# Working out the next group's mean and deviation inside the last stage of the group before it

## The chip, the cores and the metric

The kernel runs on one core of one Trainium2 chip. The metric is the device time of one launch in microseconds (us), as a median of several runs.

## The reference

Four layers follow one another on a tensor of 16 images, 32 channels, 128 x 128, in single precision. Each adds to its input the result of one operation on the group-normalised input (16 groups of two channels per image):

```python
x = x + row_lstm(_gn(x), W2, b2, W1, b1)      # layer 0: 128 steps, one per diagonal
x = x + adder_conv(_gn(x), weight)            # layer 1: -sum |patch - w| over 32 channels x 9 taps, quantised
x = x + hartley(_gn(x), weights1)             # layer 2: 2-D Hartley transform, 32 x 32 modes mixed, and back
x = x + unet(_gn(x), conv1_w, ...)            # layer 3: 5 edge operators, 7 convolutions, 3 poolings, 3 deconvolutions

def _gn(v, G=16, eps=1e-5):                   # mean and variance over 2 channels x 128 x 128
    m = jnp.mean(g, axis=(2, 3, 4)); s = jnp.var(g, axis=(2, 3, 4))
    return (g - m) / jnp.sqrt(s + eps)
```

The change concerns the mean and the deviation that layer 2 uses, that is, `m` and `1/sqrt(s + eps)` of the output of layer 1.

## The kernel before, in words

`stage0` (L103) is layer 0. It ends about 650 us into the profiled execution. `rest` (L493) then runs three things in one stream of instructions.

The first is the adder convolution, `Differences.run` (L682). It goes over 16 images and two halves of each; a half takes 72 tiles of 128 x 8192 differences. A tile is made either on VectorE (DVE, `d_dve`, L760) or on ScalarE (ACT, `d_act`, L757), whichever would be free earlier by the planned durations `DVE_US` and `ACT_US` (L487), and TensorE (PE) sums it (L647). At the end of a half, `finish` (L624) adds the residual and writes the partial statistics `stat` (L630) that layer 2 needs; when both halves of an image `b` are stored, `weave.finished = b` (L636).

The second is the background: layers 2 and 3 for groups of four images, in `After.work` (L975). Group `g` may start when `weave.finished` has reached `4 * g + 3`. Its steps are `forward` (L1031: statistics, Hartley transform forward, mixing of the modes), `encoder` (L1511: `back`, which is the transform back; `statistics` of the edge operators; the folded table `wf` of the first convolution, L1545 to L1557; `conv1`, L1683; then small layers), and `last` (L1794: the last composed deconvolution, the multiplication by the residual, and the store of the output in 16 transfers per unit of rows, L1847).

These are Python generators, and the order of the instructions on every engine is fixed while the program is written. `Weave` (L351) holds a planned clock. A positive number yielded is planned TensorE time; a negative one is a wait of so many planned us before the generator goes on; `SUMMED` is a wait until the products before it are done. While such a wait runs, only adder tiles are put into the queues. `later` puts a step off by some planned us, `done` runs it at once. The queues themselves are in order: an instruction that has to wait for data holds up everything behind it on its engine, and the queue of SyncE (SP), which issues most transfers, runs as far ahead as its own waits let it.

The third is the end. After the last adder tile, `drain` (L455) interleaves what is left of group 2 (the first `Weave`, groups 0 to 2) with all of group 3 (a second `Weave` with its own memory and PSUM banks). Waits are stretched by 1.5 in it, until one of the two streams is through; the other is then `alone`.

At the boundary between two groups the planned waits are these. `last` ends with `yield -16.0` (L1879) and then stores whatever is not stored yet (L1880). `work` waits 8 more (L981). `forward` then zeroes `xs` on ACT (L1044), issues four loads of `xh` (L1053, 1 MB each), aggregates the statistics (L1059), and calls `normalised` (L780), which sends two tiny products through TensorE (L786, L795) and takes an inverse square root in 19 small VectorE instructions (L802 to L814). A third product (L1069) spreads the result over all partitions, two VectorE instructions (L1071, L1074) leave it in `mr`, and after `yield -4.0` (L1111) the first product of the transform (L1119) reads `xh`. `mr` is used by `scaled` (L1079, L1082).

Of the kernel before, what the change touches and what calls it, by code (L numbers as in the profile page):

```python
# [7 lines left out]
F32 = mybir.dt.float32  # L8
# [3 lines left out]
ALU = mybir.AluOpType  # L12
# [3 lines left out]
B, C, H, W = 16, 32, 128, 128  # L16
# [334 lines left out]
class Weave:  # L351
# [10 lines left out]
    def __init__(self, work):  # L362
        self.work, self.pending = work, None
        self.pe = self.dve = self.act = self.now = self.base = 0.0
        self.until = self.ready = 0.0
        self.draining = self.alone = False
        self.stretch = 1.0
        self.finished, self.count, self.put_off, self.for_act, self.ends = -1, 0, [], [], {}
# [121 lines left out]
SUMMED = ("summed",)  # L490
# [289 lines left out]
def normalised(nc, pool, ps, weave, mv, n, avg, eps, out):  # L780

    mean = pool.tile([128, n], F32, name="ns_mean")
    nc.vector.tensor_copy(mean, mv[:, :, 0])
    yield -2.0
    p = ps.tile([128, 512], F32, name="acc")
    nc.tensor.matmul(p[:, :n], avg, mean, start=True, stop=True)  # L786
    yield SUMMED
    nc.vector.tensor_copy(out[:, 0], p[:, :n])
    v = pool.tile([128, n], F32, name="ns_v")
    nc.vector.tensor_sub(v, mean, out[:, 0])  # L790
    nc.vector.tensor_mul(v, v, v)
    nc.vector.tensor_add(v, v, mv[:, :, 1])
    yield -2.0
    p = ps.tile([128, 512], F32, name="acc")
    nc.tensor.matmul(p[:, :n], avg, v, start=True, stop=True)  # L795
    yield SUMMED
    nc.vector.tensor_copy(v, p[:, :n])
    inv_sqrt_into(nc, pool, weave, out[:, 1], v, n, eps)
    yield -2.0


def inv_sqrt_into(nc, pool, weave, out, v, n, eps):  # L802

    a = pool.tile([128, n], F32, name="is_a")
    nc.vector.tensor_scalar(a, v, eps, None, ALU.add)
    i = pool.tile([128, n], I32, name="is_i")
    nc.vector.tensor_scalar(i, a.bitcast(I32), 1, None, ALU.arith_shift_right)
    nc.vector.tensor_scalar(i, i, -1.0, 1597463007.0, ALU.mult, ALU.add)
    y, t = i.bitcast(F32), pool.tile([128, n], F32, name="is_t")
    for k in range(4):  # L810
        nc.vector.tensor_mul(t, y, y)
        nc.vector.tensor_mul(t, t, a)
        nc.vector.tensor_scalar(t, t, -0.5, 1.5, ALU.mult, ALU.add)
        nc.vector.tensor_mul(out if k == 3 else y, y, t)  # L814
    weave.dve += 2.0
# [143 lines left out]
class After:  # L959


    def __init__(self, nc, tc, side, sm, ps, cst, bias, a, d, stat, out):
        self.nc, self.tc, self.side, self.ps, self.cst, self.bias = nc, tc, side, ps, cst, bias
        self.a, self.d, self.stat, self.out = a, d, stat, out
        self.spare, self.banks = None, 0
        self.buffers = {"t_x": 4, "xm": 3, "xw": 2, "t_w": 3, "t_r": 4, "frames": 2, "gm": 3, "e_v": 3, "l_x": 2}
        store = [d["up"][i] for i in range(3)]
        self.up5 = Composed(nc, sm, a, "deconv1", "conv5", bias[:, 7:8], bias[:, 4:5], store[0])
        self.up6 = Composed(nc, sm, a, "deconv2", "conv6", bias[:, 8:9], bias[:, 5:6], store[1])
        self.up7 = Composed(nc, sm, a, "deconv3", "conv7", bias[:, 9:10], bias[:, 6:7], store[2])  # L970
# [4 lines left out]
    def work(self, groups):  # L975
        if 0 in groups:
            yield from self.prepare()
        for g in groups:
            with self.pool("g_sm") as sm:
                yield ("after", 4 * g + 3)  # L980
                yield -8.0  # L981
                self.stats3 = sm.tile([128, 2, 1], F32, name="stats3")
                self.shift3 = sm.tile([128, 1], F32, name="shift3")
                yield from self.forward(g)
                with ExitStack() as kept:
                    yield from self.encoder(g, kept)
                    yield from self.last(g)

    def acc(self):

# [40 lines left out]
    def forward(self, g):  # L1031

        nc, tc, cst, d, weave = self.nc, self.tc, self.cst, self.d, self.weave
        x2, xm_d, z_d = d["x2"], d["xm"], d["z"]
        ahead = self.buffers["t_x"]
        with self.pool("t_m") as mp:
            mr = mp.tile([128, 2, 4, C], F32, name="mr")


            xs = mp.tile([128, 8, 16, 32], F32, name="xs")  # L1040
            for part, off in ((slice(0, 64), xs[:64, 4:]), (slice(64, 128), xs[64:, :4])):
                one = cst["ones"][part, 0:1]
# [3 lines left out]
            with self.pool("t_t") as tp, ExitStack() as rows:  # L1046
                xp = rows.enter_context(self.pool("t_x", ahead))

                def load(n):

                    xh = xp.tile([128, 16, W], F32, name="xh")
                    first = x2.offset + (4 * g + n // 2) * CHW + 16 * (n % 2) * HW
                    nc.sync.dma_start(xh, bass.AP(x2.tensor, first, [[W, H], [HW, 16], [1, W]]))  # L1053
                    return xh

                xh = [load(n) for n in range(ahead)]
                mv = tp.tile([128, 4, 2], F32, name="mv2")
                for i in range(4):
                    nc.vector.bn_aggr(mv[:, i, :], self.stat[:, 4 * g + i].rearrange("p a b -> p (a b)"))  # L1059
                both = tp.tile([128, 2, 4], F32, name="both2")  # L1060
                yield from normalised(nc, tp, self.ps, weave, mv, 4, cst["avg8_jc"], 1e-5, both)

                diag = tp.tile([32, 8, C], F32, name="diag")
                nc.vector.tensor_tensor(
                    diag, bcast(cst["ident"][:32, :], 1, 8), bcast(both[:32].rearrange("p a b -> p (a b)"), 2, C), ALU.mult
                )
                yield -2.0
                p = self.acc()
                nc.tensor.matmul(p[:, :256], cst["ones"][:32, :], diag.rearrange("p b c -> p (b c)"), start=True, stop=True)  # L1069
                yield SUMMED  # L1070
                nc.vector.tensor_copy(mr.rearrange("p a b c -> p (a b c)"), p[:, :256])  # L1071


                nc.vector.scalar_tensor_tensor(mr[:, 0], mr[:, 0], float(H), mr[:, 1], ALU.mult, ALU.mult)  # L1074

                def scaled(n, p):
                    cs = slice(16 * (n % 2), 16 * (n % 2) + 16)
# [78 lines left out]
                for n in range(8):  # L1156
                    while steps[n]:
                        weave.done(steps[n])
                yield from self.mixing(g, xs, wp, wt)

    def modes(self, g, b, pool, xs, steps):

# [628 lines left out]
        for v in spreads:  # L1791
            weave.done(v)

    def last(self, g):  # L1794

        nc, tc, cst, weave = self.nc, self.tc, self.cst, self.weave
        with self.pool("l_y") as yp, self.pool("l_x", self.buffers["l_x"]) as xp:
# [21 lines left out]
            p = self.acc()  # L1819
# [38 lines left out]
            for unit in range(4):  # L1858
# [17 lines left out]
                        weave.dve += 0.75  # L1876
                    yield -2.5
                following[unit] = weave.on_act(lambda x=x, unit=unit: done(x, unit))
            yield -16.0  # L1879
            for unit in range(4):  # L1880
                complete(unit)

# [161 lines left out]
```

## Time and profile before

| | us |
|---|---|
| median of 3 runs | 6719.5 (6713.72 to 6728.77) |
| the profiled execution, own time | 6728.15 |
| its span | 6726.4 |
| layer 0 and its statistics | to about 650 |
| adder tiles, with groups 0, 1, 2 in the background | 685 to 5602 |
| group 2 and group 3 interleaved | 5602 to 6423 |
| group 3 alone | 6423 to 6726 |

Starts of the same step in the four groups, from the instructions of each line:

| step | group 0 | group 1 | group 2 | group 3 |
|---|---|---|---|---|
| aggregate statistics, L1059 | 1808.6 | 3401.9 | 4997.9 | 5622.1 |
| `mr` done, L1074 | 1830.9 | 3425.7 | 5021.6 | 5661.1 |
| first product of the transform, L1119 | 1837.4 | 3433.5 | 5028.5 | 5665.9 |
| statistics of the operators, L1420 | 2239.6 | 3834.1 | 5433.6 | 6037.8 |
| first convolution, L1739 | 2476.2 | 4073.8 | 5667.7 | 6247.0 |
| end of the last VectorE step, L1868 | 3376.6 | 4972.5 | 6414.3 | 6714.9 |

A share of busy time on the page is a mean over the whole span: in the adder part VectorE and ScalarE are both nearly full, in the end neither is. So the views by window, where each stage stands for itself, are the ones to read. In a line of the timeline the first number is the start, the second the length, and a bracket gives the idle time before it and what ended it.

### The profile page before, as it was taken

To read this page: it belongs to the slowest core of one execution; us is meant where nothing else is said; L and a number is where in the kernel's file an instruction comes from. 1 tells how busy PE (TensorE), PEld (TensorE's weight loads), DVE (VectorE), ACT (ScalarE), POOL (GpSimd) and SP (SyncE) were. 2 spreads that over 40 slices of the span, in tenths; PEclk is the share of its full clock that TensorE was granted. 3 is DMA by queue.
4 is the path that set the end of the run, shared out by engine and by line. 5 is a ranking of instruction groups with operands and counts; after the bars stand their busy time and mean duration, and the time that the engine had idled before them with its cause. 6 is when DMAs were issued, how large, how long until landed. Compare 5 with 4: busy or idle time off the path is not lost.

```text
span 6726.4 us, 271378 instructions
## 1 busy us (share of the span) xinstructions
PE 5379.0 (80%) x127212; PEld 2798.3 (42%) x127212; DVE 5537.9 (82%) x6839; ACT 5464.8 (81%) x3210; POOL 63.0 (1%) x67
## 2 busy tenths in 40 slices
PE   3798777788777879997877878998787785886896
PEld 3675333333343433333333433333334442453574
DVE  7898999999999889998999989999899995144122
ACT  3998999999999989999999999999899993121112
POOL 0000000000000000000000000000000000000000
PEclk9999899999989989998999889999899897997897
DMA  7553312212253632213453552221354353355314
GB/s 318 204 190 123 81 49 64 61 31 66 71 140 113 178 94 60 62 38 72 101 147 93 174 149 68 66 63 42 87 128 138 103 155 119 125 188 141 83 39 107
DMA packets 380776, 728.20 MB, mean 108 GB/s; under 512 B 73284, under 2 KB 225348, under 8 KB 368772
## 3 DMA queue, kind: packets, MB, share of 16 engines
q1 hardware_dynamic: 372180, 676.41, 35.2%
q0 software_dynamic: 7040, 33.80, 1.5%
q8 instruction: 995, 16.30, 1.0%
q14 instruction: 129, 1.06, 0.1%
q10 hardware_dynamic: 432, 0.64, 0.0%
HBM read 510.69 MB, written 200.00 MB: 106 GB/s over the span
## 4 chain that ended last, share of the span: by engine, by line
issue 33%; PE 29%; DVE 20%; ACT 14%; DMA 3%; SPq 1%; POOL 0%; DVEq 0%; ACTq 0%; POOLq 0%
DVE d_dve L760 12%; PE acc L1739 11%; ACT d_act L757 9%; PE acc L647 8%; PE acc L905 3%; PE pg L223 3%; ACT gt L237 2%; DMA v<-fold_d 1%; PE acc L1589 1%; PE acc L1420 1%; ACT junk L198 1%; DVE y L1677 1%; DVE stat L124 1%; DMA x_in<-in_x_dram 1%; ACT th L247 1%
## 5 line engine op out<-in xcount | busy, mean ns | idle before, releaser
L757 ACT ACTIVATE d_act<-q,neg 128x8192 f16<-128x8192 f16 (+1 forms) x629 | 4450.5, 7154 | 102.7 <-PE acc L647 81.1
L760 DVE TENSOR_SCALAR d_dve<-q,qw 128x8192 f16<-128x8192 f16 (+1 forms) x1675 | 3864.3, 2360 | 214.5 <-PE acc L647 195.6
L647 PE MATMUL acc<-d_dve,sel 128*32 128x512 f16 x26800 | 1879.4, 404 | 436.3 <-DVE d_dve L760 344.6
L647 PEld LDWEIGHTS <-sel 128*32 128x32 f16 x36864 | 1021.0, 101 | 2124.4 <-issue 1475.8
L1739 PE MATMUL acc<-xp,wf 32*32 32x512 f32 x25600 | 1001.7, 611 | 32.6 <-issue 27.2
L647 PE MATMUL acc<-d_act,sel 128*32 128x512 f16 x10064 | 740.0, 416 | 345.2 <-ACT d_act L757 333.4
L1680 ACT ACTIVATE y<-pooled,b 32x128 f32<-32x128 f32 x472 | 188.7, 400 | 552.6 <-DVE pooled L1666 546.3
L1739 PEld LDWEIGHTS acc<-xp,wf 32*32 32x32 f32 x25600 | 417.6, 104 | 377.6 <-issue 295.8
L677 PE MATMUL acc<-q,zero 128*32 128x512 f16 x6720 | 484.2, 400 | 0.0
L905 PE MATMUL acc<-y,u_conv 32*32 32x256 f32 (+1 forms) x9728 | 358.7, 461 | 85.1 <-issue 68.7
L223 PE MATMUL pg<-h,wb 64*64 64x20 f32 (+15 forms) x8192 | 342.0, 306 | 58.0 <-DVE h L251 32.9
L237 ACT ACTIVATE gt<-pg,bias 128x20 f32<-128x20 f32 (+15 forms) x1024 | 332.7, 385 | 39.3 <-PE pg L223 37.1
L223 PEld LDWEIGHTS pg<-h,wb 64*64 64x64 f32 x8192 | 252.1, 151 | 133.5 <-DVE h L251 80.9
L677 PEld LDWEIGHTS <-zero 128*32 128x32 f16 x6720 | 200.6, 101 | 187.3 <-issue 42.7
L1868 DVE SCALAR_TENSOR_TENSOR xr<-acc,l_one,xr 128x512 f32<-128x512 f32 x128 | 87.2, 744 | 229.8 <-PE acc L905 179.7
L1420 PE MATMUL acc<-xp 32*64 32x204 f32 (+3 forms) x8576 | 240.8, 339 | 40.6 <-issue 40.5
L905 PEld LDWEIGHTS acc<-y,u_conv 32*32 32x32 f32 x9728 | 162.0, 109 | 216.9 <-issue 168.1
L1420 PEld LDWEIGHTS acc<-xp 32*64 32x64 f32 (+1 forms) x8576 | 169.1, 132 | 124.4 <-issue 118.9
L1838 ACT ACTIVATE xr<-xr,l_ms 128x1024 f32<-128x1024 f32 x64 | 68.7, 1146 | 182.1 <-DVE xr L1868 171.9
L223 PE MATMUL pg<-xn,wb 64*64 64x2 f32 (+63 forms) x4096 | 183.5, 290 | 25.6 <-issue 17.0
L1774 DVE TENSOR_TENSOR acc<-acc,cut 128x4 f32<-128x4 f32 x256 | 35.2, 164 | 200.6 <-PE acc L1739 198.3
L1589 PE MATMUL acc<-y,w_conv 32*32 32x512 f32 (+2 forms) x4608 | 153.6, 487 | 37.1 <-issue 28.9
(218 smaller groups left out, 3624.5 us busy)
## 6 DMA issues: line engine op xcount, KB each, us to landing
q<-q_d SPq DMA_DIRECT2D x128, 536.2 KB, 10.3
xp<-xn_d SPq DMA_DIRECT2D x64, 660.0 KB, 5.1
xp<-x_d SPq DMA_DIRECT2D x56, 640.0 KB, 5.3
xr<-xn_d SPq DMA_DIRECT2D x64, 528.0 KB, 11.3
x_in<-in_x_dram SPq DMA_DIRECT2D x16, 2048.0 KB, 14.7
xn<-in_xs_dram SPq DMA_DIRECT2D x64, 512.0 KB, 7.1
res<-in_x_dram SPq DMA_DIRECT2D x64, 512.0 KB, 8.6
x_d<-res SPq DMA_DIRECT2D x64, 512.0 KB, 4.8
```

The source lines that it names most:

```text
L223: nc.tensor.matmul(bank[c][q][64 * pair : 64 * pair + 64, :, :width], wb[half, 4 * kind + KIND[q]].rearrange("p b o -> p (b o)"), v[half], ...
L237: nc.scalar.activation(gt[:, q, :, :n], bank[c][q][:, :, :n], AF.Tanh if q == G else AF.Sigmoid, bias=bias[:, KIND[q] : KIND[q] + 1],)
L647: self.nc.tensor.matmul(acc[k][32 * j : 32 * j + 32, :], self.sel16[:, i // 9, :], d[:, row : row + 4, c : c + W], start=first, stop=last,)
L677: self.nc.tensor.matmul(acc[k][32 * j : 32 * j + 32, :], self.zero, q[:, :4, :W], start=False, stop=False)
L757: nc.scalar.activation(dst, src, AF.Relu, bias=self.neg[:, i : i + 1])
L760: nc.vector.tensor_scalar(dst, src, self.qw[:, i : i + 1], 0.0, ALU.subtract, ALU.max)
L905: nc.tensor.matmul(acc[blk][32 * j : 32 * j + 32, o : o + rows * n], t[part, 4 * par + tap, :], src[part, top : top + rows, left : left + ...
L1420: nc.tensor.matmul(gram[blk][j : j + width, at : at + n], xp[part, l, 2 + j : 2 + j + width], xp[part, rows, j : j + width + 4], start=sta ...
L1589: nc.tensor.matmul(acc[blk][32 * j : 32 * j + 32, : rows * n], wc[name][part, tap, :], src[part, at : at + rows, kw : kw + n], start=tap == 0,
L1680: nc.scalar.activation(d, s, AF.Identity, bias=bj)
L1739: nc.tensor.matmul(acc[blk][32 * j : 32 * j + 32, :], tap_of("all", tap)[rows], xp[rows, 4 * j + kh : 4 * j + kh + 4, kw : kw + W], start= ...
L1868: nc.vector.scalar_tensor_tensor(v, acc[blk].rearrange("p (b r w) -> p r w b", b=2, w=64), one[:, blk : blk + 1], v, ALU.add, ALU.mult,)
```

## The change

The statistics of layer 2 move into a function of their own, `scaling`. `last` is told which group follows in the same stream. If that group's four images are finished when `last` has emitted its products, `last` runs `scaling` for it in the place of `yield -16.0`; `work` then leaves out its wait of 8 for that group, and `forward` takes `mr` from a dictionary. Where nothing was prepared (the first group, and group 3, which has a stream of its own), `forward` runs `scaling` where it stood. `mr` lives in the pool that is kept throughout, in two buffers, and no longer in `t_m`; the small tiles of `scaling` are taken from the pool of `last`. [...]

```diff
@@ work @@
                 yield ("after", 4 * g + 3)
-                yield -8.0
+                if g not in self.scales:
+                    yield -8.0
...
-                    yield from self.last(g)
+                    yield from self.last(g, g + 1 if g + 1 in groups else None)
@@ forward @@
-            mr = mp.tile([128, 2, 4, C], F32, name="mr")
...
                 xh = [load(n) for n in range(ahead)]
-                mv = tp.tile([128, 4, 2], F32, name="mv2")
...
-                nc.vector.scalar_tensor_tensor(mr[:, 0], mr[:, 0], float(H), mr[:, 1], ALU.mult, ALU.mult)
+                if g not in self.scales:
+                    yield from self.scaling(g, tp)
+                mr = self.scales.pop(g)
@@ new @@
+    def scaling(self, g, pool):
+        nc, cst, weave = self.nc, self.cst, self.weave
+        mr = self.sm.tile([128, 2, 4, C], F32, name="mr", bufs=2)
+        mv = pool.tile([128, 4, 2], F32, name="mv2")
+        for i in range(4):
+            nc.vector.bn_aggr(mv[:, i, :], self.stat[:, 4 * g + i].rearrange("p a b -> p (a b)"))
+        both = pool.tile([128, 2, 4], F32, name="both2")
+        yield from normalised(nc, pool, self.ps, weave, mv, 4, cst["avg8_jc"], 1e-5, both)
+        diag = pool.tile([32, 8, C], F32, name="diag")
+        nc.vector.tensor_tensor(
+            diag, bcast(cst["ident"][:32, :], 1, 8), bcast(both[:32].rearrange("p a b -> p (a b)"), 2, C), ALU.mult
+        )
+        yield -2.0
+        p = self.acc()
+        nc.tensor.matmul(p[:, :256], cst["ones"][:32, :], diag.rearrange("p b c -> p (b c)"), start=True, stop=True)
+        yield SUMMED
+        nc.vector.tensor_copy(mr.rearrange("p a b c -> p (a b c)"), p[:, :256])
+        nc.vector.scalar_tensor_tensor(mr[:, 0], mr[:, 0], float(H), mr[:, 1], ALU.mult, ALU.mult)
+        self.scales[g] = mr
@@ last @@
-            yield -16.0
+            if following_group is not None and weave.finished >= 4 * following_group + 3:
+                yield from self.scaling(following_group, yp)
+            else:
+                yield -16.0
             for unit in range(4):
                 complete(unit)
@@ kernel @@
-    nc = bacc.Bacc("TRN2", target_bir_lowering=False, num_devices=1)
+    nc = bacc.Bacc("TRN2", target_bir_lowering=False, num_devices=1, dynamic_dma_scratch_size=4096)
```

More of the change, by code (lines that the diff above doesn't have):

```diff
@@ L965, in __init__ @@
         self.spare, self.banks = None, 0
+        self.sm, self.scales = sm, {}
         self.buffers = {"t_x": 4, "xm": 3, "xw": 2, "t_w": 3, "t_r": 4, "frames": 2, "gm": 3, "e_v": 3, "l_x": 2}
@@ L1056, in forward @@
                 xh = [load(n) for n in range(ahead)]
-                mv = tp.tile([128, 4, 2], F32, name="mv2")
[L1058 to L1074, printed above, removed]
+                if g not in self.scales:
+                    yield from self.scaling(g, tp)
+                mr = self.scales.pop(g)
                 def scaled(n, p):
@@ L1792, in conv1, with last @@
             weave.done(v)
-    def last(self, g):
+    def last(self, g, following_group):
         nc, tc, cst, weave = self.nc, self.tc, self.cst, self.weave
```

## The prediction

> **What bounds the kernel now.** I read the page's slices first, then the busy time by window, then the timeline at the boundary between groups 0 and 1 and at the end of the adder part.
>
> The busy times by window, from the end of the adder part on (columns: length; busy time and number of instructions of PE, PEld, DVE, ACT, POOL; granted clock; share and rate of the transfers):
>
> ```profile
> 5602.00:5667.00 65.00, 14.28 (x736) 10.18 (x735) 30.11 (x77) 3.94 (x3) 3.73 (x7) 0.50 0.74 229
> 5667.00:6018.00 351.00, 316.90 (x9203) 167.79 (x9202) 100.99 (x267) 44.81 (x112) 2.66 (x5) 0.97 0.40 126
> 6018.00:6247.00 229.00, 147.21 (x5008) 88.89 (x5001) 91.40 (x284) 45.08 (x82) 5.28 (x10) 0.77 0.48 146
> 6247.00:6423.00 176.00, 152.74 (x5237) 104.77 (x5225) 29.22 (x65) 36.38 (x64) 0.00 (x0) 0.93 0.39 97
> 6423.00:6543.00 120.00, 119.05 (x3785) 100.67 (x3760) 22.06 (x80) 12.80 (x32) 0.00 (x0) 1.00 0.06 18
> 6543.00:6726.00 183.00, 120.71 (x4402) 80.44 (x4385) 59.85 (x140) 47.56 (x80) 0.00 (x0) 0.80 0.46 105
> ```
>
> Up to 5602 VectorE and ScalarE are full with adder tiles (from 3396 to 4993, a whole group, they are busy 1481.63 and 1532.66 of 1597 us), so the adder part is a sum of VectorE and ScalarE work. After it TensorE is the fullest engine. Its one large hole is the first 65 us, busy 14. Why it is empty there:
>
> ```profile
> 5602.84 2.73 DVE L628 SCALAR_TENSOR_TENSOR xr<-acc,sumw,xr 128x512 f32<-128x512 f32 x4 [3.19 <-PE acc L647]
> ...
> 5610.34 1.97 DVE L1551 TENSOR_SCALAR wf<-v,ops 128x1440 f32<-128x1440 f32 x3
> ...
> 5640.94 1.85 DVE L1553 SCALAR_TENSOR_TENSOR wf<-v,ops,wf 128x1152 f32<-128x1152 f32 x2 [1.91 <-DMA v<-fold_d]
> ...
> 5667.72 2.87 PE L1739 MATMUL acc<-xp,wf 32*32 32x512 f32 x49
> ```
>
> The adder part ends (L628) just as group 2 starts to build its table `wf`, 57 us short of its first convolution, and group 3 has only begun to load. Neither has products to offer.
>
> The boundary after group 0:
>
> ```profile
> 3373.84 2.72 DVE L1868 SCALAR_TENSOR_TENSOR xr<-acc,l_one,xr 128x512 f32<-128x512 f32 x4
> ...
> 3396.46 11.76 SPq L1053 DMA_DIRECT2D xh<-x_d  x4
> ...
> 3401.95 1.06 DVE L1059 BATCH_NORM_AGGREGATE mv<-stat 128x2 f32<-128x48 f32 x4
> ...
> 3425.37 0.29 DVE L1074 SCALAR_TENSOR_TENSOR mr<-mr 128x128 f32<-128x128 f32 x1
> ...
> 3433.69 1.88 PE L1119 MATMUL acc<-xh,cw 128*32 128x512 f32 x16
> ```
>
> From the last multiplication's end (3376.6) to the first product of the next group 57 us pass, and the adder tiles run through all of it. So the boundary costs no adder time; it only holds the background back.
>
> [...] L811, on four elements, takes a median 161 ns, and the inverse square root's 19 such instructions last from 3415.3 to 3419.1. [...] 0.50 granted in the empty 65 us, 0.97 in the full window behind it. [...] The longest burst in the trace is 5 `gm` and 6 `v` (6002.6 to 6022.6), so the smaller scratch should cost nothing; no run shows it. If it did, L1553 would wait longer for `v`; it waits 23.1 us in all now, and I keep up to 5 more for it.
>
> **The change, part by part.** It acts twice, after groups 0 and 1; group 2 has no successor in its stream, and group 3 has its own. The condition holds: before 3373 17 halves have passed L628 (16 needed), before 4969 27 (24 needed).
>
> Removed at each boundary: the planned waits 16 and 8. On the chip they stand as 3376.6 to 3401.95, 25.4 us, and as 4972.5 to 4997.9, 25.4 us, of which 2.5 is a wait that stays. So `mr` should be done some 23 us earlier, near 3403 and 4999. The 23.7 us of the statistics themselves (3401.95 to 3425.66) are moved, not removed; the same instructions, the same three products, no transfer among them; POOL's queue is not passed. Two buffers of `mr`, the small tiles and the dictionary cost nothing: nobody waits for them.
>
> Added: the loads of `xh` lose their cover. They now stand behind the statistics in program order, so only the wait of 4 and what the planner puts between hide them: 7.8 us from L1074 to L1119 before, against 8.2 us from the first load's issue (3396.46) to its landing (3404.6). SP doesn't wait for the statistics, only for what stands ahead: output stores, `x2` stores, `xq`, and now also `q` (4.7 us at 3408.3). With SP free at 3396.3, `q` would end near 3401, the first load land near 3409, and the product be due near 3411. I take 1 us each; 0 to 5 are possible, not less than 0, since nothing goes sooner than planned. TensorE in order holds the adder's sums meanwhile, and three `d_dve` buffers of 2.35 us cover most of it. The output stores themselves stay as they were: SP waits for ACT there.
>
> So group 2 is ahead by 2 x 22 = 44 us when the adder part ends. What it then does sooner is taken from group 1's same stretch. At 5602 group 2 stood where group 1 stood at 4009; 44 us on is 4053. Building `wf` (14.0 + 2.0 us), the rest of the inverse square root and small copies make 19 us of VectorE work up to 4069. This moves out of the empty stretch into the full adder part. VectorE makes 1675 of 2304 tiles, 0.73, so sharing between the two engines costs 19 x 0.73 = 14 us; with 4 for stalls and sums behind the loads, the adder part's last VectorE step ends at 5626 and not 5608. Both ends: 0 (VectorE's idle 10.5 us in that stretch takes it in) to 27.
>
> With those 18 us group 2 is just at its first convolution: 5626 and not 5667.7. Group 3 starts at 5608 + 18 = 5626; its first product came 58 us later before, of which 15 us (5645 to 5660) were L1069 standing behind group 2's L1713; I take 50: 5676, 10 late.
>
> From there by rates. The first convolution has 6400 products a group: 18.2 per us beside group 3 (351 us), 31.3 per us alone (3118 in 99 us at 6440). From 5626 to 5676 group 2 has TensorE almost to itself: at 25 per us, half way between the two rates, 1250 are done, the other 5150 at 18.2 take 283: end 5959, 59 sooner. I take 50 for the end of group 2, since its small layers then meet group 3's transform back: 6361 and not 6411. Group 3 is 8 late at its own convolution: 6255. It shares until 6361, at 16 per us (2807 in 176 us): 1700; the other 4700 at 31.3 take 150: 6511 and not 6543. The tail (183 us) is unchanged. **Sum:** 32 sooner; I say 30: a span near 6696 against 6726.4, its execution 6698 against 6728.15, which lay 8.65 above the median. On the median: 6719.5 - 30 = 6689.5.
>
> **The rivals.** *Nothing comes back:* group 3's own chain of waits decides. For it: TensorE is idle for 202 us after 5667, so not every product gained is time gained. Then the 18 us of the adder part, less the 8 to 15 us at L1069, less some 5, leave 6715 to 6725; say 6718. *All comes back:* TensorE decides. The hole of 51 us goes, and the 14 us of its own work move into the adder part; less the 18, 47 sooner, up to 55 if the adder grows less: 6670. Against it: the same idle time. *Slower:* the 19 us of VectorE work now lie in the full part, and group 3 meets a dense first convolution from its first step, so each of its small steps waits behind a tap of 32 products (about 1 us at 31.3 per us); group 2's lead fills holes that nobody needed. The 18 us, up to 7 for such steps, against under 8 won: 17 later, 6736. It decides where group 3 gets back less than the adder part loses. *The change doesn't act*, if the planner's `finished` lags the trace: excluded with one half image to spare at the first boundary; 6719.5.
>
> **How the numbers follow.** Forecast 0.54; all comes back 0.11; nothing comes back or no action 0.17; slower 0.18. What a measurement of this kernel tells from no change is about 0.2%, 13 us. Faster takes the first two: 0.65; within 0.17; slower 0.18. The range goes from 6664 (all comes back, adder growing less) to 6735, into the slower case; about 0.1 lies above and under 0.1 below. The forecast's own range is 6675 to 6706.
>
> **What would show it.** Right: `mr` near 3403 and 4999, first products 20 to 24 us sooner; last L628 at 5620 to 5635; `wf` built before it; first convolution of group 2 near 5626 with the clock near 1 there; group 3's convolution near 6255. Wrong: L1119 waiting on transfers with L760 idle behind it; L628 unmoved or over 5640; group 3's convolution after 6270.

## The result, and the profile after

| | before | after |
|---|---|---|
| median | 6718.8 us (6713.7 to 6728.8, 4 runs) | 6660.9 us (6656.7 to 6671.8, 4 runs) |
| the profiled execution, own time | 6728.15 | 6656.74 |
| its span | 6726.4 | 6655.0 |
| ratio of the times | 1 | 0.9915, 95% interval 0.9897 to 0.9932 |

The change saves 58 us of the medians (46 to 69 by the interval), where 30 were forecast. The two profiled executions differ by 71, because that of before lay above its median and that of after was the fastest of its runs: about 13 us of any difference read from these two traces is chance.

The boundary after group 0 in the changed kernel (L1876 was L1868, L1151 was L1059, L1855 was L1847, L1052 was L1053, L1166 was L1074, L1103 was L1119):

```profile
3372.24 2.72 DVE L1876 SCALAR_TENSOR_TENSOR xr<-acc,l_one,xr 128x512 f32<-128x512 f32 x4
3374.88 1.05 DVE L1151 BATCH_NORM_AGGREGATE mv<-stat 128x2 f32<-128x48 f32 x4
3380.06 8.79 SPq L1855 DMA_DIRECT2D out_dram<-xr  x16
3397.61 10.44 SPq L1052 DMA_DIRECT2D xh<-x_d  x4
3400.14 0.29 DVE L1166 SCALAR_TENSOR_TENSOR mr<-mr 128x128 f32<-128x128 f32 x1
3405.65 0.35 PEld L1103 LDWEIGHTS acc<-xh,cw 128*32 128x32 f32 x8
```

The statistics start with the end of the last multiplication, the output leaves while they run, and the first product comes 27.8 us sooner. It now follows the loads of `xh` and not `mr`: they leave at 3397.6, as before (3396.5), and the product comes 8.0 us later. At the second boundary 37.7 us more are won (the first product of group 2 is at 4963.0 instead of 5028.5).

The end of the adder part, as it was shown of before:

```profile
5588.15 2.73 DVE L628 SCALAR_TENSOR_TENSOR xr<-acc,sumw,xr 128x512 f32<-128x512 f32 x4 [1.50 <-PE acc L647]
...
5593.43 7.14 PE L1747 MATMUL acc<-xp,wf 32*32 32x512 f32 x135 [4.40 <-DVE cut L1733]
```

The table `wf` is built before the adder part ends, and the first convolution (L1747, was L1739) starts 5 us behind the start of the last L628 instead of 65. The windows show the hole gone (same columns as before: length; PE, PEld, DVE, ACT, POOL; clock; share and rate of the transfers):

```profile
5588.00:5593.00 5.00, 1.03 (x46) 0.40 (x38) 4.85 (x8) 0.00 (x0) 0.00 (x0) 0.85 0.50 134
5593.00:5940.00 347.00, 322.50 (x9182) 171.19 (x9184) 98.24 (x273) 48.62 (x114) 0.00 (x0) 0.95 0.44 140
5940.00:6200.00 260.00, 173.42 (x5649) 109.87 (x5646) 106.49 (x320) 49.39 (x86) 7.94 (x15) 0.76 0.56 163
6200.00:6324.00 124.00, 110.24 (x3820) 74.30 (x3821) 20.90 (x48) 25.70 (x44) 0.00 (x0) 0.96 0.36 90
6324.00:6472.00 148.00, 147.49 (x4583) 122.24 (x4573) 27.68 (x100) 16.00 (x40) 0.00 (x0) 1.00 0.08 26
6472.00:6655.00 183.00, 119.32 (x4390) 82.70 (x4379) 59.85 (x140) 47.52 (x80) 0.00 (x0) 0.80 0.46 105
```

The 65 us with TensorE at 14 have become 5; the tail of group 3 is the same 183 us. From the last L628 to the end 1066.9 us pass instead of 1123.6: 57 us won there. But the last L628 itself is not 18 us late, as forecast; in these two traces it is 15 us early. What the adder part contains shows why it isn't late, in one window from 3231 to the end of L628, before and then after:

```profile
3231.00:5605.60 2374.60, 1962.09 (x44122) 911.74 (x44121) 2217.95 (x1899) 2291.38 (x603) 30.96 (x23) 0.92 0.40 108
```
```profile
3231.00:5590.90 2359.90, 1936.40 (x44382) 900.50 (x44381) 2237.16 (x1934) 2286.45 (x602) 38.04 (x30) 0.92 0.41 111
```

VectorE is busy 19.2 us more (2217.95 to 2237.16; one adder tile of 2.4 us is among it): the work that I said would move in did. Yet the stretch is 14.7 us shorter, since VectorE's idle time in it fell from 156.7 to 122.7 (length less busy). On the page the whole kernel's line says the same, before and after:

```profile
L760 DVE TENSOR_SCALAR d_dve<-q,qw 128x8192 f16<-128x8192 f16 (+1 forms) x1675 | 3864.3, 2360 | 214.5 <-PE acc L647 195.6
```
```profile
L760 DVE TENSOR_SCALAR d_dve<-q,qw 128x8192 f16<-128x8192 f16 (+1 forms) x1676 | 3865.2, 2362 | 165.1 <-PE acc L647 146.1
```

VectorE waits for TensorE to sum a tile and give its buffer back, 50 us less in all.

How much of this is chance? The table of runs in the next section gives an estimate. In the seven kernels whose second boundary is as it was (before, e2, f1, h1, e4, e7, f2) the last L628 starts anywhere from 5582 to 5609, but from there to the end of the span it is always 1121 to 1125 us. And of the 8.4 us between the two profiles of the changed kernel (after and f3), 6.3 lie ahead of the last L628. So the chance of a profile lies mostly in the adder part. With it taken off, the last L628 stands at 5593.4 before (that profile was 9.4 us above its kernel's median) and at 5592.3 after (4.2 below): level. So most of the 15 us are chance, and some 20 of the 34 us of idle time are left, about as much as the work that moved in.

Where did VectorE idle less? Half by half, the largest part lies in two of them, which hold group 1's transform back, its `wf` table and its edge tables (L1713; L1721 after). Before, then after; 36.5 us idle become 18.3 (20.9 in the second profile of the change; 32.7 and 38.1 in e2 and e4, kernels of the next section whose background has no lead):

```profile
3860.30:4042.20 181.90, 139.66 (x3271) 71.10 (x3264) 160.30 (x180) 165.96 (x53) 9.55 (x9) 0.84 0.50 144
4042.20:4191.80 149.60, 134.94 (x3317) 54.50 (x3310) 134.68 (x86) 140.71 (x39) 0.00 (x0) 0.91 0.24 62
```
```profile
3858.90:4029.60 170.70, 129.43 (x3302) 66.88 (x3283) 157.37 (x176) 162.91 (x47) 9.50 (x9) 0.87 0.46 138
4029.60:4171.10 141.50, 131.78 (x3116) 53.39 (x3114) 136.50 (x88) 141.29 (x39) 0.00 (x0) 1.00 0.26 65
```

The edge tables are 704 products of 32 x 32. Before, they began at 4039.1, 3 us ahead of the change from one half to the next (L628 at 4042.2), and took 31 us. After, they ran from 4011.8 to 4031.5, all but the last 2 us ahead of the change (L628 at 4029.6), and took 20. This is TensorE's timeline before, its waits for nothing but `issue`, and VectorE behind it:

```profile
4044.25 1.38 PE L1713 MATMUL acc<-sides,wf 32*32 32x32 f32 x113 [1.92 <-issue]
4048.54 0.33 PE L1713 MATMUL acc<-cw,wf 32*32 32x32 f32 x12 [2.77 <-issue]
...
4063.16 1.25 PE L1713 MATMUL acc<-sides,wf 32*32 32x32 f32 x101 [6.44 <-issue]
```
```profile
4066.29 2.38 DVE L760 TENSOR_SCALAR d_dve<-q,qw 128x8320 f16<-128x8320 f16 x1 [6.75 <-PE acc L647]
```

For 6.44 us TensorE idles and waits for no data and no buffer that the profile shows; VectorE runs out of free tiles for 6.75 us. At this change of a half SyncE sends the stores of `x2`, the loads of `xq` and of `q` (4043.7 to 4054.8), and the transfer engines are busy 0.92 of the time from 4044 to 4064. The page lists loads of instructions among the transfers (packets, MB, their time as a share of the span of 16 engines):

```profile
q8 instruction: 995, 16.30, 1.0%
```

The line is that of before; after has 992 packets and 16.25 MB. Divided by TensorE's products and weight loads (254.4 and 253.5 thousand) that is 64 bytes each in both kernels. My theory, inferred from these sums: the packets are TensorE's instructions, they are held up when the 16 engines are full, and a stretch of many tiny products uses them up fastest (in the tables of after TensorE runs 872 products in 19.9 us, 44 a us, against 19 a us over the span of before). In the records of queue 8 the packets, of 16 KB each, came at 4041.5, 4046.2, 4050.7 and then 4060.4, against one each 3.5 us in the undisturbed tables of after, where the engines were busy 0.02 of the time.

### The profile page after: what moved, and what is told of

Same layout as the page of the kernel before. It is cut to its first block, busy times and chain, and to the rows that moved or that the text cites. A ratio compares the mean times of both kernels' runs of the same rounds, so it can differ in the third digit from the quotient of the medians.

```text
span 6655.0 us, 270517 instructions
## 1 busy us (share of the span) xinstructions
PE 5351.9 (80%) x126760; PEld 2793.3 (42%) x126760; DVE 5541.6 (83%) x6848; ACT 5455.3 (82%) x3201; POOL 66.4 (1%) x67
## 3 DMA queue, kind: packets, MB, share of 16 engines
q8 instruction: 992, 16.25, 1.0%
## 4 chain that ended last, share of the span: by engine, by line
issue 33%; PE 29%; DVE 21%; ACT 13%; DMA 4%; SPq 1%; POOL 0%; DVEq 0%; ACTq 0%; POOLq 0%
DVE d_dve L760 12%; PE acc L1747 11%; ACT d_act L757 8%; PE acc L647 7%; PE pg L223 3%; PE acc L905 3%; ACT gt L237 2%; PE acc L1597 1%; DVE stat L124 1%; DVE y L1685 1%; ACT junk L198 1%; PE acc L1428 1%; DMA v<-fold_d 1%; DMA xm_d<-xm 1%; ACT th L247 1%
## 5 line engine op out<-in xcount | busy, mean ns | idle before, releaser
L647 PE MATMUL acc<-d_dve,sel 128*32 128x512 f16 x26816 | 1874.2, 403 | 491.2 <-DVE d_dve L760 392.6
L647 PEld LDWEIGHTS <-sel 128*32 128x32 f16 x36864 | 1010.6, 100 | 2118.9 <-issue 1461.4
L1747 PE MATMUL acc<-xp,wf 32*32 32x512 f32 x25600 | 1000.9, 610 | 26.0 <-issue 17.5
L647 PE MATMUL acc<-d_act,sel 128*32 128x512 f16 x10048 | 734.1, 414 | 292.4 <-ACT d_act L757 285.3
L1747 PEld LDWEIGHTS acc<-xp,wf 32*32 32x32 f32 x25600 | 422.7, 104 | 373.1 <-issue 292.5
L677 PE MATMUL acc<-q,zero 128*32 128x512 f16 x6268 | 449.3, 399 | 0.0
L905 PE MATMUL acc<-y,u_conv 32*32 32x256 f32 (+1 forms) x9728 | 339.0, 453 | 88.5 <-issue 66.8
L237 ACT ACTIVATE gt<-pg,bias 128x20 f32<-128x20 f32 (+15 forms) x1024 | 332.3, 384 | 40.1 <-PE pg L223 38.1
L1876 DVE SCALAR_TENSOR_TENSOR xr<-acc,l_one,xr 128x512 f32<-128x512 f32 x128 | 87.1, 743 | 199.0 <-PE acc L905 131.3
## 6 DMA issues: line engine op xcount, KB each, us to landing
x_in<-in_x_dram SPq DMA_DIRECT2D x16, 2048.0 KB, 14.7
```

The costliest lines, as they stand in the source:

```text
L237: nc.scalar.activation(gt[:, q, :, :n], bank[c][q][:, :, :n], AF.Tanh if q == G else AF.Sigmoid, bias=bias[:, KIND[q] : KIND[q] + 1],)
L647: self.nc.tensor.matmul(acc[k][32 * j : 32 * j + 32, :], self.sel16[:, i // 9, :], d[:, row : row + 4, c : c + W], start=first, stop=last,)
L677: self.nc.tensor.matmul(acc[k][32 * j : 32 * j + 32, :], self.zero, q[:, :4, :W], start=False, stop=False)
L905: nc.tensor.matmul(acc[blk][32 * j : 32 * j + 32, o : o + rows * n], t[part, 4 * par + tap, :], src[part, top : top + rows, left : left + ...
L1747: nc.tensor.matmul(acc[blk][32 * j : 32 * j + 32, :], tap_of("all", tap)[rows], xp[rows, 4 * j + kh : 4 * j + kh + 4, kw : kw + W], start= ...
L1876: nc.vector.scalar_tensor_tensor(v, acc[blk].rearrange("p (b r w) -> p r w b", b=2, w=64), one[:, blk : blk + 1], v, ALU.add, ALU.mult,)
```

## The experiments

A table first, for reference. Times within a kernel are from its one profile; "rule" is explained behind it.

| run | ratio to before | last L628 starts | conv1 of group 2 starts | rule | span |
|---|---|---|---|---|---|
| before | 1 | 5602.8 | 5667.7 | 6728 | 6726 |
| after | 0.9915 | 5588.1 | 5593.4 | 6655 | 6655 |
| f3_after_again | 0.9918 | 5594.4 | 5599.7 | 6661 | 6663 |
| e1_cut_waits | 0.9944 | 5627.7 | 5603.7 | 6695 | 6695 |
| e2_put_back | 0.9993 | 5589.6 | 5651.8 | 6712 | 6712 |
| e3_second_only | 0.9965 | 5626.1 | 5635.9 | 6696 | 6707 |
| f1_first_only | 0.9974 | 5582.0 | 5643.4 | 6703 | 6707 |
| h1_first_then_pause | 0.9969 | 5582.0 | 5646.3 | 6706 | 6706 |
| e6_tables_late | 0.9931 | 5625.6 | 5632.9 | 6693 | 6696 |
| f4_pause_behind | 0.9948 | 5597.1 | 5623.7 | 6684 | 6692 |
| e5_q_later | 0.9931 | 5604.6 | 5609.9 | 6672 | 6685 |
| e8_more_lead | 0.9967 | 5645.3 | 5655.7 | 6716 | 6709 |
| h2_group0_ahead | 0.9914 | 5614.3 | 5589.3 | 6681 | 6681 |
| h3_forward_kept | 0.9914 | 5604.4 | 5580.5 | 6671 | 6673 |
| e4_scratch | 1.0002 | 5606.9 | 5670.8 | 6731 | 6728 |
| e7_before_q_later | 1.0000 | 5603.4 | 5667.5 | 6728 | 6724 |
| f2_before_q_wait | 1.0007 | 5609.2 | 5673.6 | 6734 | 6732 |

The rule came out of the runs and was not in the prediction: the end is the later of two things, the last L628 plus 1067 us and the start of group 2's first convolution plus 1060. So it is a description of these runs, not a forecast that was tested. The two constants are from after (1066.9) and from before and after (1058.7, 1061.6). It meets the other fifteen spans within 14 us, eleven of them within 4. It says that a lead is worth something until the convolution starts 7 us behind the adder part, and nothing beyond.

For the adder part alone, the chance of each profile can be taken off as above: the last L628, less what its profile lay above its own median, compared with before's, which is put 1125 us (6728.15 less 5602.8) ahead of the median that before had beside that run. These are estimates, each good to about the interval of its ratio, 5 to 12 us:

| run | its profile less its median | last L628 against before's |
|---|---|---|
| after | -4 | -1 |
| f3_after_again | -11 | +3 |
| h3_forward_kept | 0 | -5 |
| e2_put_back | -9 | -4 |
| e3_second_only | +3 | +20 |
| f1_first_only | -1 | -20 |
| h1_first_then_pause | -5 | -23 |
| e6_tables_late | +9 | +8 |
| f4_pause_behind | 0 | -5 |

**Each boundary alone, and the waits put back.** One line of the changed kernel decides each:

```diff
@@ e2: last, behind the scaling @@
+                yield -24.0
@@ e3: last (f1 has == 1) @@
-            if following_group is not None and
+            if following_group == 2 and
```

> The changed kernel with a planned wait of 24 put in behind the statistics, at both boundaries. If only the lead counts, the background stands where it stood before and the time goes back to 6719, within 8, with the last adder step near 5603. If the moved statistics or the freed memory bring something of their own, a time under 6705 stays.

> The changed kernel acting at the second boundary alone; everything up to 4970 is the kernel before. Theory of the prediction: group 2 leads by about 28, the last adder step comes 8 to 12 later than 5603 because work on the table moves in, the end comes 15 to 25 sooner: near 6698. Theory of alignment (the adder part got shorter in the changed kernel because group 1's stages fell otherwise against the halves of an image): the last adder step isn't sooner than 5603 here, for group 1 is as before. If the second boundary alone makes it sooner, by 10 or more, alignment in group 1 isn't the cause.

> Only group 1 is prepared early; group 2's boundary is as before. Group 2 is then some 28 us ahead at the end of the adder part, as in the run with only group 2 prepared. My theory (the adder part is shorter because group 1's edge-table products no longer lie on the change of a half): those products take about 20 us instead of 31, the last L628 stands at 5585 to 5600, and the ratio is 0.993 to 0.9955. Rival (only the lead counts, whichever boundary it comes from): the last L628 near 5620 and the same ratio as with group 2 alone, 0.9965.

Put back, the gain is gone: 0.9993 (0.9986 to 1.0000). Its profile lay 9 us below the median of its runs, hence the early L628 in the table. So moving the statistics by itself is worth next to nothing; the planned waits that go are worth the rest. The second boundary alone gives 0.9965 (0.9952 to 0.9978), and its trace is just what I had forecast of the whole change: the adder part's last step at 5626.1 (20 us later than before's by the estimate), VectorE's idle time 167.7 and not below before's, the convolution 10 us behind. The first boundary alone gives 0.9974 (0.9964 to 0.9984) in another way: the last L628 starts at 5582.0, 21 us early (20 by the estimate) as my theory had it, and the convolution stands 61 us behind it, nearly as before. The ratio missed the 0.993 to 0.9955 of my theory: I had counted a lead of 28 on top, but against the adder part only 3.5 us of it were left (61.4 us behind instead of 64.9).

**The place of group 1's stretch.** h1 prepares group 1 early and gives the time back behind its edge tables:

```diff
-            if following_group is not None and
+            if following_group == 1 and
@@ conv1, behind the edge tables @@
+        if g == 1:
+            yield -28.0
```

> Only group 1 is prepared early, and what it gained is given back by a wait of 28 behind its edge tables, so that the first convolution of group 1 and all of group 2 stand as in the kernel before, and only the tables of group 1 have moved off the change of a half. My theory (the tables' place made the adder part shorter; the end is set by the later of two things, the adder's end plus 1067 and the start of group 2's first convolution plus 1060): idle time of VectorE in the two halves around the tables about 20 us instead of 36, last L628 at 5585 to 5595, first convolution of group 2 at 5660 to 5670, and in spite of the shorter adder part the ratio is 0.999 to 1.001. Rival (a shorter adder part is time gained by itself): ratio 0.997 to 0.998. Second rival (the place of the tables is not what did it): last L628 near 5603.

Idle time in the two halves:

```profile
3854.40:4027.40 173.00, 129.21 (x3312) 66.77 (x3312) 157.40 (x176) 163.56 (x47) 9.49 (x9) 0.87 0.46 137
4027.40:4170.70 143.30, 129.96 (x2882) 56.02 (x2879) 136.50 (x87) 143.05 (x40) 0.00 (x0) 0.95 0.26 64
```

That is 15.6 and 6.8, 22.4 instead of 36.5; the last L628 starts at 5582.0, 21 us early (23 by the estimate). Here my theory was right on the place and wrong on the worth: I expected no gain, since the convolution would start where it did before. It started 21 us sooner too. The background's plan runs on the adder's clock, so a shorter adder part brings everything behind it forward. The ratio is 0.9969 (0.9956 to 0.9981), 21 us: the first rival's number. So moving group 1's stretch against the changes of the halves is worth about 21 us with no lead at all. The stretch is moved as a whole here: that it is the changes of the halves that it has to avoid, and nothing else about the earlier place, this run doesn't show.

**The tables pushed back onto the change, and the same pause behind them.**

```diff
@@ e6: behind the loop that builds wf, ahead of the edge tables @@
+            if g == 1:
+                yield -15.0
@@ f4: conv1, behind the edge tables @@
+        if g == 1:
+            yield -15.0
```

> The changed kernel with a wait of 15 put ahead of the edge-table products in group 1 alone, so that they start about 3 before the change of a half, as in the kernel before. Collision theory: they take 31 instead of 20, idle 9 to 11 for instructions instead of 2, the two halves around them lose 12 to 18, and the last adder step comes 5 to 15 later than 5588; time near 6670. Rival (the lead alone makes the adder part shorter): 15 less lead, less work moves in, the adder step comes up to 6 sooner.

> After, with the same wait of 15 for group 1 as in the run that pushed its edge tables back, but behind the tables and ahead of the taps of the first convolution: group 2 loses the same planned time, and the tables stay where they are in after. My theory: tables about 20 us, last L628 at 5590 to 5610, ratio 0.9915 to 0.9925, 4 or more us better than with the wait ahead of the tables (0.9931). Rival (that run's loss was the lead's 15 us alone): the same 0.9931, and last L628 near 5625 as there.

In the adder part the pair goes the way of the theory: with the tables on the change (34 us long) the last L628 starts at 5625.6 and VectorE idles 158.4 us; with the same pause behind them (20 us long) at 5597.1 and 131.1. By the estimate only 13 of these 28 us are more than chance (+8 and -5), hardly more than its error. In the time it does not: 0.9931 (0.9915 to 0.9948) against 0.9948 (0.9934 to 0.9961), the other way round, with intervals that overlap. The rule offers a reason: in f4 the convolution starts 27 us behind the last L628 and sets the end, in e6 7 us behind. Read so, a shorter adder part that group 2 can't follow is not collected.

**What fills the transfer engines at the change.** Three runs move the load of `q` away:

```diff
@@ e5 (in after), e7 (in before) @@
-                    if i == 8 and (b, half) != (B - 1, 1):
+                    if i == 24 and (b, half) != (B - 1, 1):
@@ f2 (in before): behind a store that SyncE must wait for @@
+                    if i == (8 if half else 36) and (b, half) != (B - 1, 1):
```

> The changed kernel with the adder's load of the next half's rows (q, 2.1 MB) moved from its tile 8 to its tile 24, away from the stores and loads at the change of a half. Collision theory (TensorE's instruction loads are held up when the edge-table products of conv1 meet the transfers at the change of a half): group 0, whose table products still meet them in the changed kernel, idles 3 us for instructions in them instead of 12.5, the last adder step comes 8 to 15 sooner than 5588, the time 6650. Rival, that where the background lies against the tiles makes the difference and not the transfers: no change beyond 4.

> The kernel before with the load of q moved from tile 8 to tile 24, and no lead at all. Collision theory: the table products of groups 0 and 1 take 20 to 24 instead of 31, VectorE's idle time in the two halves around each falls by 8 to 15, the last adder step comes 15 to 28 sooner than 5603, the time falls by 15 to 25. Rival (lead): unchanged within 5.

> Before, with the load of q in an image's first half put behind the store of the first quantised tile, for which SyncE has to wait, so that it can no longer leave at the change of a half. My theory (a burst of transfers at the change of a half starves the edge-table products): the tables of groups 0 and 1 take 20 to 25 us instead of 31, the last L628 comes 10 to 20 us sooner, ratio 0.997 to 0.9985. Rival (q is not what does it; the x2 stores and xq are enough, or the place has another cause): tables still 29 to 32 us, ratio 1.000.

e5 and e7 (0.9931, 0.9917 to 0.9946, beside after's 0.9915; and 1.0000, 0.9992 to 1.0009) tell little: SyncE runs ahead of the plan, so the load moved in its queue and hardly in time (in e7 it left at 4044.9, 9.1 us behind the first store of the change, in before at 4049.9, 6.2 behind). f2 did move it, to 4097.4. Transfers and waits in 25 us from just before the change on, before and then f2:

```profile
DMA packets 965, 4.38 MB, mean 175 GB/s; under 512 B 320, under 2 KB 320, under 8 KB 832
q8 instruction: 5, 0.08, 1.4%
```
```profile
DMA packets 775, 2.21 MB, mean 89 GB/s; under 512 B 256, under 2 KB 256, under 8 KB 768
q8 instruction: 7, 0.11, 2.1%
```
```profile
4046.45 1.39 PE L1713 MATMUL acc<-sides,wf 32*32 32x32 f32 x113 [2.00 <-issue]
4050.75 0.33 PE L1713 MATMUL acc<-cw,wf 32*32 32x32 f32 x12 [2.77 <-issue]
```

With half the bytes (2.21 MB instead of 4.38), two more loads of instructions come through (7 instead of 5), TensorE's wait of 6.44 is gone (the longest is now the 2.77 above), and so is VectorE's of 6.75. Group 1's tables take 24 us instead of 31. So the hole in the tables is due to the transfers, as the theory says; that the loads of instructions are the link agrees with the two more of them, and is not shown beyond that. But its worth is not what I expected: VectorE's idle time in the two halves falls only to 34.0, the adder part doesn't end sooner (5609.2), and the ratio is 1.0007 (1.0000 to 1.0015). The tables' hole alone isn't the 21 us; VectorE's idle time in these halves is 2.5 us less, so other waits have taken back some 4 of the 6.75, and the rest of the stretch (the transform back, with waits up to 8.48 us within 45 us of the change at 3860.3) was moved in h1 too, and not here.

**The place of the statistics.** Does it matter that they stand in `last`, or only that the waits are gone? Both runs leave out the two waits and keep the statistics in `forward`, behind the loads; e1 takes the tiles from `forward`'s own pool, h3 takes them and `mr` from the pool that is kept throughout.

```diff
@@ e1 (in before): last; work leaves out its 8 for that group @@
-            yield -16.0
+            if following_group is not None and weave.finished >= 4 * following_group + 3:
+                self.early.add(following_group)
+            else:
+                yield -16.0
@@ h3 (in after): the same, and in forward @@
-                    yield from self.scaling(g, tp)
+                    yield from self.scaling(g, self.sm)
```

> The kernel before with the planned waits of 16 and 8 left out at the two boundaries and the statistics left where they stood, behind the loads. If only the lead of the background counts, and not the place of the statistics, group 1's first product of the transform comes near 3406 and group 2's near 4963, as in the changed kernel, and the time is 6661, within 15. If the place counts (the statistics under the last stores), the boundary shortens by less than half as much and the time stays over 6695.

> The planned waits are left out as after, but the statistics stay in forward behind the loads, with their small tiles and mr in memory that is kept throughout, so that they wait for no store. If only the lead counts: the half at the first boundary lasts 158 to 165 us (178 with the tiles over the output buffers), last L628 at 5590 to 5600, ratio 0.991 to 0.9925. Rival (the place at the end of the last stage is worth something by itself): last L628 near 5620, ratio 0.994 as in the run with the waits cut.

e1 gives 0.9944 (0.9929 to 0.9959), two thirds of the gain. Its statistics wait 10.33 us for the output to be stored, since their small tiles lie over the memory of its buffers:

```profile
3388.00 1.06 DVE L1061 BATCH_NORM_AGGREGATE mv<-stat 128x2 f32<-128x48 f32 x4 [10.33 <-DMA out_dram<-xr]
```

ScalarE then stood 14.4 us waiting for TensorE (3397.9 to 3412.3), and the half took 178 us instead of 158. With tiles of their own, in h3, they wait for nothing:

```profile
3374.66 1.05 DVE L1151 BATCH_NORM_AGGREGATE mv<-stat 128x2 f32<-128x48 f32 x4
...
3385.47 9.78 SPq L1052 DMA_DIRECT2D xh<-x_d  x4
3395.22 0.29 DVE L1166 SCALAR_TENSOR_TENSOR mr<-mr 128x128 f32<-128x128 f32 x1
```

The half takes 165 us (161 in after), and the ratio is 0.9914 (0.9901 to 0.9928), the change's own. So the place in `last` has no worth of its own that shows. Its last L628 starts at 5604.4, no sooner than before's trace had it, and VectorE idles 141.0 us in its adder part: the whole gain is there without an adder part as short as in the trace of after. The place in `last` is one way of two to get rid of the waits without waiting for memory.

**More lead.** Two runs look for more:

```diff
@@ e8: last, ahead of the last unit of rows instead of behind it @@
+                if unit == 3 and following_group is not None and weave.finished >= 4 * following_group + 3:
+                    yield from self.scaling(following_group, yp)
@@ h2: work, and the loop that builds wf @@
-                if g not in self.scales:
+                if g not in self.scales and g:
                     yield -8.0
...
-                yield -1.2
+                yield -1.2 if g else -0.3
```

> The changed kernel with the statistics of the following group put ahead of the last unit of rows in the last stage, so that nothing but the loads is left at the boundary. If lead goes on to pay, group 2 leads by some 30 more and the end comes 15 to 20 sooner than 6655. If the empty 50 us at the start of the end part were all there was to fill, the further lead moves work into the adder part and the end stays within 8.

> After, with group 0 some 17 planned us ahead as well: its wait of 8 at the start is left out, and the waits between the pieces of the wf table are 0.3 instead of 1.2 for it. Its edge tables then end near the change of a half at 2444 instead of lying on it. If the place of the tables is what matters, and both terms of the end move together: group 0's tables take 20 to 25 us instead of 31, group 2's first convolution starts at 5573 to 5583, the last L628 stands at 5570 to 5580, ratio 0.9885 to 0.990. Rival (the gain is spent, the adder part has no more to give): last L628 at 5590 to 5600 and ratio 0.9915 to 0.9925.

e8 loses, 0.9967 (0.9954 to 0.9980): `last` itself ends 31 us later (3406.2), and the loads have lost their cover. Now TensorE does stand before the transfers, at both boundaries:

```profile
3423.30 1.93 PE L1103 MATMUL acc<-xh,cw 128*32 128x512 f32 x8 [10.32 <-DMA xh<-x_d]
...
5029.62 1.94 PE L1103 MATMUL acc<-xh,cw 128*32 128x512 f32 x8 [12.97 <-DMA xh<-x_d]
```

No sum of an adder tile (L647) ran on TensorE in those 10.3 and 13.0 us. In after TensorE's waits for the loads are 1.1 to 2.9 us: there the statistics run beside the stores of the output, and the loads leave at 3397.6 instead of 3416.6. h2 changes nothing, 0.9914 (0.9900 to 0.9927): group 0's tables still took 28.5 us on their change, the adder part ended at 5614.3 with the convolution 25 us ahead of it, and a lead that large is not collected. No run beat the change by more than its interval.

**The scratch memory alone, and the change once more.**

> The kernel before with the smaller descriptor memory and nothing else. All theories: no change, 6719 within 5. If the memory counts, L1553 waits longer for v, and the time rises.

> The changed kernel once more, for how much a second profile differs. Ratio 0.9915 within 0.001; last L628 at 5588 within 10 us; VectorE idle in the adder part 123 us within 10.

e4 sets `dynamic_dma_scratch_size` to 4096 in before, as the change does, and alters nothing else. It does nothing to the time, 1.0002 (0.9992 to 1.0011). That it would cost nothing was in the prediction an estimate of mine that nothing measured had shown; this ratio is the measurement. The change once more gives 0.9918 (0.9903 to 0.9932), with the last L628 at 5594.4 and VectorE idle 128.9 us in the adder part. But this profile was the quickest of its runs, 11 us below their median; by the estimate its adder part is as long as before's.

## Why the prediction was right in direction and short by half

- **Right: the waits were the gain, the hole was where it would show.** `mr` was forecast near 3403 and 4999; the first is 3400.4, the second 4959.2. From the adder part's end to the kernel's end I had 1070 us (5626 to 6696) and the trace has 1064 (5590.9 to 6655.0). Group 2's convolution was forecast at the adder part's end and came 3 us behind it. The granted clock was forecast near 1 there: it was 0.50 in the old hole, and is 0.95 in the full window that has taken its place.
- **Right: the moved VectorE work.** 19 us forecast, 19.2 measured with one tile more.
- **Wrong, and the step that failed:** "the adder part's last VectorE step ends at 5626 and not 5608", the 18 us by which the adder part was to grow. It ended at 5590.9 (5597.2 in the second profile); with the chance of the profiles taken off that is level with before (-1 and +3 us). The sum of moved work was right, but I took VectorE's idle time as constant, but for 4 us more. It fell by 34 and 28 us in the two traces, some 20 and 16 of them beyond chance, and so made up for the work that moved in. The lead that removed the waits had also moved group 1's transform back and tables against the changes of halves. h1 shows this part alone: 21 us gained (13 to 30), the adder part 23 us shorter. e3 shows the lead of group 2 alone, with the stretch left in place: 24 us gained (15 to 32), the adder part 20 us longer, and there my step was right. In the change both act, and 20 more with 23 less fits the level adder part. The two gains add up to 44, within the errors of the 58 that the change saves; what the rest is, if it is anything, isn't settled.
- **Mis-sized: the end part.** From the adder part's end on I had 48 us won (1118 before, 1070 after); it was 57. So of the 28 us that separate the 58 from the forecast 30, about 19 belong to the adder part and 9 to the end.
- **Mis-sized: the boundary.** "2 x 22 = 44" was 65.5 at the first product of group 2. At the first boundary the wait of 2.5 that "stays" doesn't stand ahead of the statistics (they start with the multiplication's end), and the time from `mr` to the product shrank from 7.8 to 5.2 and 3.8 us. I had excluded a gain there. At the second boundary, 7 us more came from group 1's own stretch, and 31 from the boundary. By the rule this larger lead alone would have brought nothing: with the last L628 starting at 5623, as I had it, the kernel would have ended near 6690, about my 6696.
- **The rivals:** "all comes back" (6670) was nearest in time, and for the end part it was nearly right. TensorE's idle time behind the hole stayed about the same (202 us before, 189 after), so almost the whole hole was won. Its sum fell short because it, too, had the adder part grow by 18. The 57 us of the end part rule out "nothing comes back". "Slower" did not occur; group 3's own convolution started at 6200, 55 us sooner than I had put it. L1103 waiting on transfers, which I named as a sign of failure, is real, but takes e8's order to appear.
- **Open:** how the 21 us of h1 divide between the tables and the transform back, and whether it is the changes of the halves that make the earlier place better. f2 shows that 7 of the tables' 31 us are due to the load of `q`, and that to cure this alone gains nothing measurable.

## What to carry to other kernels

When a change shifts a stage, don't only count the work that moves: look at what the stage stood beside, before and after. Here a stretch of 704 tiny products lay across a burst of transfers: TensorE stood 6.44 us in it and VectorE 6.75 waiting for it, though to halve the burst gained nothing that could be measured (1.0007). Before a difference of two profiles is explained, ask how far each lies from its kernel's median: here that was most of the 15 us. And where two streams must both arrive, price each against the later one: in these runs a lead beyond the partner's end, and a shorter part that the partner couldn't follow, both came to nothing.

## What was not expected of the hardware

- Loads of instructions stand among the transfers: 995 of 16 KB on queue 8 in before. That they are TensorE's is my inference from the 64 bytes, the same in both kernels, for each of its products and weight loads. In the tables of tiny products of after one came each 3.5 us; under the burst of transfers in before one came 9.6 us after the one before, and TensorE stood 6.44 us with no wait for data or buffers that the profile shows. With the burst halved, in f2, its longest such wait in the tables was 2.77.
- Small tiles allocated over buffers that were still being stored cost e1 10.3 us on VectorE, and ScalarE then stood 14.4 waiting for TensorE, at a place where the program names no transfer.
